# A graph layer and a mixture of experts: x also arrives transposed, and the row two edge groups share travels by DRAM

## The chip, the cores and the metric

The kernel runs on one core of one Trainium2 chip. Its time is that of one execution on the device, in microseconds (us).

## The reference, cut to what matters

The input `x` has 6250 nodes of 256 values. There are 100000 edges (`src`, `dst`), sorted by `dst`. All is float32.

```python
edge_index = jnp.stack([src, dst])
x = x + gnn(layernorm(x), edge_index, W, b)       # mean over a node's edges of h[src], then [h, mean] @ W.T + b
x = x + moe(layernorm(x)[None], ...)[0]           # norm again, 8 experts, the best 2 of them weighed by softmax

def gnn(h, edge_index, W, b):
    src, dst = edge_index
    msg_sum = segment_sum(h[src], dst, n)
    deg = segment_sum(ones, dst, n)
    agg = msg_sum / maximum(deg, 1)[:, None]
    return concatenate([h, agg], axis=1) @ W.T + b
```

## The kernel before, in words

**The start.** The nodes lie in 49 tiles of 128 rows (the last holds 106), taken in 13 blocks of four tiles (`TB`). The kernel multiplies x by the centred weights before it gathers anything: `z` is the normalised x times the half of W that the mean needs, and `u` is x plus the bias plus the normalised x times the other half. Both go to DRAM (`z_d`, `u_d`).

- `load_x` (L168) brings a block of x into `xt`, rows on the partitions; five blocks are asked for ahead, each later one after the block five before it.
- `z_statistics` (L201) takes mean and variance of each tile on DVE, 0.40 and 0.18 us each; `z_deviations` (L209) makes `rstd_x` of a block by a root on ACT (L146) and five small operations on DVE (L151 to L156).
- `z_block` (L215) handles a block in half blocks of two tiles. TensorE turns them with four transposes (L226), ACT copies the result into `x_t` (L227), and `product` (L192) multiplies `x_t` by `gc` (L197). ACT scales the product into `zt` (L237), and SP stores it in `z_d` (L240). The product of a half block is issued after the transposes of the next one (the list `pending`).
- From the fourth block on, a list of other steps is put between half blocks, one after each: constants, the second centring of weights, the turning of the edge lists into `src_i` and `dst_i`, the places of the windows (`place_windows`, `place_rows`) and checks that the edges are sorted.
- `u_stages` (L349) makes `u` in 26 tasks: load `xu`, add the bias (L356), multiply `x_t` by the other half (L197), add (L363), store (L367). Six of them stand ahead of the first edges and the others between them. `x_t` is kept until they are done.

**The edges.** The edges are cut in 784 groups of 128; 14 groups make a window, so there are 56 windows. One group is a step t of the program. POOL gathers the 128 rows of z that a group needs (`gather`, L533) into one of 16 buffers `xg`, 16 steps ahead of use. DVE compares each edge's `dst`, less the window's first node, with 0 to 127 and so makes `hot`, seven groups at once (L544, two buffers), and TensorE adds `hot` times `xg` up in `pS` (`add_edges`, L550), one product per step, with a 257th column of ones for the degree. A window covers the nodes from its first edge's on, 128 rows.

The last node of a window can have more edges in the next one; it is the next window's row 0. Before, this row goes over by a product. ACT copies `pS` into `sums` at the window's end (L556). DVE makes `move` from `last_row` (`carry`, L561), a matrix that picks the shared row and puts it in row 0, and TensorE adds `move` times the previous `sums` to `pS` after the seventh step of the window (L553). Float32 products show as two passes each in the profile.

`window_x1` (L572) divides by the degree and adds `u`, which `load_u` (L563) brings at step 13; the result goes to DRAM (L577).

**The experts.** Windows are grouped in nine chunks (4, then five of 8, then three of 4). For each chunk the tokens are normed, routed, sorted by products (L622) and copied into the experts' slots `xe` (`copy_runs` on ACT, L737, 64 copies for 8 windows). Then come 11 expert items (`expert_stages`, L753 to L810), the results go to `y_d`, and two gathers of POOL per window (L851) bring them back.

**The order.** All five queues (PE, DVE, ACT, POOL, SP) run in an order written out by hand. `after(t)` issues what is due at step t: `at(t, f)` puts a function at a step, `window_done` (L902) puts all that follows a window at fixed distances (`Steps`), and the expert tasks are spread at a rate worked out from their prices and deadlines. Each engine works through its own list in order.

Of the kernel before, what the change touches and what calls it, by code (L numbers as in the profile page):

```python
# [8 lines left out]
F32 = mybir.dt.float32  # L9
I32 = mybir.dt.int32  # L10
AF = mybir.ActivationFunctionType
ALU = mybir.AluOpType
# [5 lines left out]
P = 128  # L18
# [10 lines left out]


@with_exitstack
def gnn_ffn_kernel(ctx: ExitStack, tc: tile.TileContext, x, src, dst, gw_t, gb, gamma, beta,
                   wr, br, w1, b1, w2, b2, out):


# [52 lines left out]
    def slot_number(nw):  # L88
        return more_at(nw) + XT * P
# [6 lines left out]
    dram = ctx.enter_context(tc.tile_pool(name="dram", bufs=1, space=DRAM))  # L96
    z_d = dram.tile([HR, D], F32, name="z_d")
    u_d = dram.tile([HR, D], F32, name="u_d")
    y_d = [dram.tile([slot_number(nw), D], F32, name=f"y_d{i}") for i, (_, nw) in enumerate(chunks)]
    AR = -(-(N + EW) // P)  # L100
    x1_d = dram.tile([W * P, D], F32, name="x1_d")
# [79 lines left out]
    def rows_of(d, t0, n):  # L181
        return d[t0 * P:(t0 + n) * P, :].rearrange("(t p) d -> p t d", p=P)
# [26 lines left out]
    def z_deviations(t0):  # L209
        n = min(TB, NT - t0)  # L210
        a = small.tile([P, TB], F32, name="var_eps")
        nc.vector.tensor_scalar(a[:, :n], mvs[t0][:, :n, 1], EPS, None, op0=ALU.add)
        rsqrt(rstd_x[:, t0:t0 + n], a, root(a, n, TB), n, TB)

    def z_block(t0, pending, between):  # L215


        n = min(TB, NT - t0)
        xt, after = xts[t0], t0 + TB
        zt = early.tile([P, TB, D], F32, name="zt")  # L220
        for i in range(0, n, 2):
            m = min(2, n - i)
            pt = ps.tile([P, 2, KD, P], F32, name="pm")
            for j in range(m):
                for k in range(KD):
                    nc.tensor.transpose(pt[:, j, k, :], xt[:, i + j, k * P:(k + 1) * P], ident)  # L226
            nc.scalar.activation(x_t[:, t0 + i:t0 + i + m], pt[:, :m], AF.Copy)  # L227
            if t0 == i == 0:
                z_deviations(0)
            if after in blocks:  # L230
                z_statistics(after, range(i, i + 2))

            def rest(i=i, m=m):
                pz = product(t0 + i, m, KD)
                for j in range(m):
                    t = t0 + i + j
                    nc.scalar.activation(zt[:, i + j, :], pz[:, j, :], AF.Identity, scale=rstd_x[:, t:t + 1])  # L237
                if i + m == n or t0 >= blocks[-3]:
                    i0 = i if t0 >= blocks[-3] else 0
                    nc.sync.dma_start(rows_of(z_d, t0 + i0, i + m - i0), zt[:, i0:i + m, :])  # L240
            if pending:
                pending.pop()()
            pending.append(rest)
            if between:
                between.pop(0)()
        if after in blocks:
            z_deviations(after)
# [55 lines left out]


    start_i = edges.tile([1, W], I32, name="start_i")
    bases = edges.tile([P, 2, W + 1], F32, name="bases")
    last_row = edges.tile([P, W], F32, name="last_row")
    token = edges.tile([P, W], F32, name="token")
    tail_i = edges.tile([P, 2], I32, name="tail_i")
    wrongs = const.tile([1, 1], F32, name="wrongs")  # L310
# [1 line left out]
    def place_windows():  # L312
        rows = early.tile([1, 2, W + 1], F32, name="rows", bufs=1)
        nc.vector.tensor_copy(rows[:, 0, :W], base_i)
        nc.vector.memset(rows[:, 0, 0:1], 0.0)
        nc.vector.memset(rows[:, 0, W:], float(N))
        nc.vector.memset(rows[:, 1, W:], 0.0)
        nc.vector.tensor_tensor(rows[:, 1, :W], rows[:, 0, 1:], rows[:, 0, :W], op=ALU.subtract)

        furthest = early.tile([1, W], F32, name="furthest", bufs=1)  # L320
        nc.vector.tensor_scalar(furthest, cols[0:1, :W], float(P - 1), float(N - P), op0=ALU.mult, op1=ALU.min)
        nc.vector.tensor_tensor(start_i, rows[:, 0, :W], furthest, op=ALU.min)
        pb = ps.tile([P, 2, W + 1], F32, name="py", bufs=1)
        nc.tensor.matmul(pb, ones[0:1, :], rows, start=True, stop=True)
        nc.vector.tensor_copy(bases, pb)

    def place_rows():
        nc.vector.tensor_scalar(last_row, bases[:, 1, :W], lane, None, op0=ALU.is_equal)
        nc.vector.tensor_scalar(token, bases[:, 1, :W], lane, None, op0=ALU.is_gt)

        tail_f = early.tile([P, 2], F32, name="tail_f", bufs=1)
        nc.vector.tensor_tensor(tail_f[:, 0:1], bases[:, 0, W - 1:W], lane, op=ALU.add)
        nc.vector.tensor_scalar(tail_f[:, 1:2], tail_f[:, 0:1], float(N - 1), None, op0=ALU.min)
        nc.vector.tensor_copy(tail_i, tail_f)
# [51 lines left out]
        return [lambda t=t: step(t) for t in range(len(pairs) + 1)]  # L386

    blocks = list(range(0, NT, TB))
    pending = []
    mvs = {}  # L390
    base_i = early.tile([1, W], I32, name="base_i", bufs=1)
    xts = {t0: load_x(early, "xt", t0, min(TB, NT - t0), TB, 6) for t0 in blocks[:5]}
    edge_parts = load_edges()
    gb_sb = u_pool.tile([P, D], F32, name="gb_sb", bufs=1)
    nc.sync.dma_start(gb_sb, bass.AP(tensor=gb.tensor, offset=gb.offset, ap=[[0, P], [1, D]]))
# [14 lines left out]
    zero = u_pool.tile([CAP, D], F32, name="zero", bufs=1)  # L410
    nc.vector.memset(zero, 0.0)
# [135 lines left out]
    def add_edges(V, c):  # L547
        if c == 0:
            V.pS = ps.tile([P, DA], F32, name="pS")
        nc.tensor.matmul(V.pS, V.hot[c // HC][:, c % HC, :], xg[(V.g * C + c) % XG],  # L550
                         start=(c == 0), stop=(c == C - 1))
        if c == HC - 1 and V.g > 0:
            nc.tensor.matmul(V.pS, V.move, V.before.sums, start=False, stop=False)  # L553
# [437 lines left out]
    for index, (first, nw) in enumerate(chunks):  # L991
# [3 lines left out]
        for g in range(first, first + nw):  # L995
# [163 lines left out]
```

## Time and profile before

| | us |
|---|---|
| median of three runs | 1258.45 (1257.22, 1258.45, 1260.78) |
| the profiled execution | 1257.93 |
| its span | 1256.2 |
| PE busy | 1127.6 (90%) |
| POOL busy | 865.4 (69%) |
| DVE busy | 672.2 (54%) |
| ACT busy | 478.6 (38%) |
| first and last gather of z start (L533) | 76.6 and 1089.6 |
| last product of edges starts (L550) | 1115.6 |

The granted TensorE clock was 0.954 of full speed on average. The profile tells for each line and engine how long it was busy, how long the engine stood idle before it, and what ended that idle time. An arrow points to the releaser: `PE ph L753 <- ACT xe L737` says that TensorE waited at line 753 for what ACT wrote at line 737. PEld is the loading of weights into TensorE, which overlaps its products. SP works only by issuing transfers and has no busy time. An engine's busy share leaves out what lies between two of its instructions, and a busy share over the whole span mixes stages with different limits.

### The profile page before, as it was taken

What the parts mean: (1) busy time and instruction counts of PE and PEld (TensorE: products, weight loads), DVE (VectorE), ACT (ScalarE), POOL (GpSimd) and SP (SyncE); (2) the same over time, 40 slices, a digit from 0 to 9 for tenths busy, and PEclk for the clock granted to TensorE, in tenths of its full rate; (3) what the DMA queues carried; (4) which work ended last, traced back from release to release, by engine and by line L of the source; (5) the groups of instructions that cost most, each with busy time, mean ns of one, the idle gap of its engine ahead of it and who ended that gap; (6) DMA issues with size and microseconds to landing.
All of it is one profiled execution on the core that took longest, in us unless ns stands there. A gap on an engine that the chain in (4) does not pass through costs nothing. (4 is left out here: it accounts for less than half of the span.)

```text
span 1256.2 us, 18368 instructions
## 1 busy us (share of the span) xinstructions
PE 1127.6 (90%) x5322; PEld 931.6 (74%) x5322; DVE 672.2 (54%) x2072; ACT 478.6 (38%) x1209; POOL 865.4 (69%) x911
## 2 busy tenths in 40 slices
PE   8888877888988999899998999899998999998782
PEld 6777744665656888688877888688877888877661
DVE  6856547353663447453563457443663646357541
ACT  5510013521165234733364333733365243533510
POOL 2047777777777777777777777777777777656652
PEclk9999978899888999899998999899999999999986
DMA  8569894444444454445444444444444555467673
GB/s 266 162 213 324 264 358 124 122 125 127 138 126 122 134 151 131 143 127 152 134 144 128 140 146 134 142 133 142 135 147 140 158 167 158 138 178 211 192 211 92
DMA packets 129682, 203.46 MB, mean 162 GB/s; under 512 B 21997, under 2 KB 98561, under 8 KB 129448
## 3 DMA queue, kind: packets, MB, share of 16 engines
q0 software_dynamic: 43104, 117.72, 33.1%
q1 hardware_dynamic: 79528, 75.59, 18.5%
q10 hardware_dynamic: 6944, 8.91, 2.1%
q8 instruction: 45, 0.74, 0.2%
q14 instruction: 61, 0.50, 0.1%
HBM read 155.84 MB, written 46.33 MB: 161 GB/s over the span
## 5 line engine op out<-in xcount | busy, mean ns | idle before, releaser
L533 POOL DMA_INDIRECT xg<-z_d,src_i x784 | 747.7, 954 | 298.3 <-issue 110.0
L550 PE MATMUL pS<-xg,hot 128*128 128x257 f32 x1568 | 439.4, 397 | 33.5 <-DMA xg<-z_d,src_i 30.2
L550 PEld LDWEIGHTS pS<-xg,hot 128*128 128x128 f32 x1568 | 293.9, 196 | 113.9 <-DMA xg<-z_d,src_i 61.9
L753 PE MATMUL ph<-xe,w_sb 128*128 128x256 f32 (+1 forms) x1152 | 224.8, 346 | 28.4 <-ACT xe L737 26.7
L753 PEld LDWEIGHTS ph<-xe,w_sb 128*128 128x128 f32 x1152 | 188.9, 199 | 50.3 <-ACT xe L737 29.5
L768 PE MATMUL py<-w_sb,hid 128*128 128x256 f32 x896 | 215.3, 385 | 6.7 <-DVE rows L772 6.7
L544 DVE TENSOR_TENSOR hot<-cols,rel 128x896 f32<-128x896 f32 x112 | 121.9, 1089 | 144.1 <-PE pS L550 140.2
L768 PEld LDWEIGHTS py<-w_sb,hid 128*128 128x128 f32 x896 | 171.8, 193 | 32.0 <-DVE rows L772 8.1
L760 ACT ACTIVATE hid<-ph,b_sb 128x256 f32<-128x256 f32 (+1 forms) x288 | 103.4, 426 | 224.3 <-PE ph L753 224.1
L737 ACT ACTIVATE xe<-xs x448 | 139.3, 311 | 57.9 <-ACT xe L737 35.9
L851 POOL DMA_INDIRECT xg<-y_d,rows_i x90 | 87.0, 967 | 64.3 <-issue 16.4
L772 DVE TENSOR_TENSOR rows<-py,b_sb 128x512 f32<-128x512 f32 x56 | 38.6, 688 | 127.2 <-PE py L768 127.2
L197 PE MATMUL ph<-gc,x_t 128*128 128x256 f32 x392 | 95.5, 389 | 12.1 <-DVE u_t L363 8.7
L625 ACT ACTIVATE xs<-pm,beta_sb,gamma_sb 128x256 f32<-128x256 f32 x112 | 57.2, 561 | 96.1 <-PE pm L622 95.5
L556 ACT ACTIVATE sums<-pS 128x257 f32<-128x257 f32 x56 | 21.7, 388 | 188.3 <-PE pS L550 134.5
L197 PEld LDWEIGHTS ph<-gc,x_t 128*128 128x128 f32 x392 | 73.9, 194 | 24.5 <-DVE u_t L363 10.1
L622 PE MATMUL pm<-to,xn 128*128 128x256 f32 x224 | 58.9, 386 | 3.6 <-DVE end L685 2.6
L858 DVE SCALAR_TENSOR_TENSOR xg<-xg,w,xg 128x256 f32<-128x256 f32 x90 | 42.8, 483 | 35.1 <-DMA xg<-x_d 21.1
L803 PE MATMUL py<-w_sb,hid 128*128 x216 | 53.5, 392 | 5.9 <-ACT hid L797 4.6
L785 PE MATMUL ph<-w_sb,xe 128*128 x108 | 53.1, 615 | 4.3 <-DVE rows L789 3.8
L622 PEld LDWEIGHTS pm<-to,xn 128*128 128x128 f32 x224 | 42.5, 192 | 12.3 <-issue 5.6
L803 PEld LDWEIGHTS py<-w_sb,hid 128*128 128x128 f32 x216 | 41.0, 195 | 13.7 <-ACT hid L797 6.0
(178 smaller groups left out, 975.9 us busy)
## 6 DMA issues: line engine op xcount, KB each, us to landing
y_d<-rows SPq DMA_DIRECT2D x56, 256.0 KB
xg<-z_d,src_i POOLq DMA_INDIRECT x784, 2.8
w_sb<-w_dram ACTq DMA_DIRECT2D x16, 512.0 KB
x_d<-x SPq DMA_DIRECT2D x56, 128.0 KB
x<-u_d SPq DMA_DIRECT2D x55, 128.0 KB
xu<-x_dram SPq DMA_DIRECT2D x24, 256.0 KB
u_d<-u_t SPq DMA_DIRECT2D x24, 256.0 KB
xg<-x_d SPq DMA_DIRECT2D x45, 128.0 KB
```

Of the source, the lines that this page charges most:

```text
L197: nc.tensor.matmul(pz[:, i, :], x_t[:, t0 + i, k, :], gc[:, k0 + k, :], start=(k == 0), stop=(k == KD - 1))
L533: nc.gpsimd.indirect_dma_start(out=xg[(g * C + c) % XG][:, :D], out_offset=None, in_=z_d[:, :], in_offset=bass.IndirectOffsetOnAxis(ap=src ...
L544: nc.vector.tensor_tensor(hot, col[:, None, :].to_broadcast([P, HC, P]), V.rel[:, c:c + HC, None].to_broadcast([P, HC, P]), op=ALU.is_equal)
L550: nc.tensor.matmul(V.pS, V.hot[c // HC][:, c % HC, :], xg[(V.g * C + c) % XG], start=(c == 0), stop=(c == C - 1))
L622: nc.tensor.matmul(px[:, k, :], G.xn[i][:, k * P:(k + 1) * P], G.one_hot[i], start=True, stop=True)
L625: nc.scalar.activation(xs[:, at:at + 2 * P], px[:, k, :], AF.Identity, bias=beta_sb[:, k:k + 1], scale=gamma_sb[:, k:k + 1])
L737: nc.scalar.activation(K.xe[:, :, bass.ds(v[2 * i], CAP)], src[:, :, bass.ds(src_at, CAP)], AF.Copy)
L753: nc.tensor.matmul(ph[:, i, a * S:(a + 1) * S], w1_sb[:, U.e + a, k, c * P:(c + 1) * P], K.xe[:, k, (U.e + a) * S:(U.e + a + 1) * S], star ...
L760: nc.scalar.activation(U.hid[:, c, a * S:(a + 1) * S], ph[:, i, a * S:(a + 1) * S], AF.Gelu, bias=b1_sb[:, U.e + a, c:c + 1])
L768: nc.tensor.matmul(U.py[:, h, :], U.hid[:, c, h * P:(h + 1) * P], w2_sb[:, U.e + h * UE // 2, c, :], start=(c == 0), stop=(c == KH - 1))
L803: nc.tensor.matmul(py[:, 0, :], T.hid[:, c, :P], w2_sb[:, bass.ds(T.e, 1), c, :].rearrange("p a d -> p (a d)"), start=(c == 0), stop=(c == ...
L851: nc.gpsimd.indirect_dma_start(out=V.y2[r], out_offset=None, in_=y_d[K.index][:, :], in_offset=bass.IndirectOffsetOnAxis(ap=G.rows[:, r, i ...
```

## The change

The host hands over a second copy of x, `x_cols`, in which each 128x128 block of x is transposed; it is the same data in another order. `x_t` is loaded from it, 512 KB per block, beside the load of `xt`. The transposes and ACT's copies out of PSUM are gone, and so is `pending`: a half block's product, scaling and store follow each other. Loads run four blocks ahead instead of five, and `zt` has three buffers instead of two. The first block's deviations come ahead of its products.

`carry`, `last_row` and the product L553 are gone. At a window's end DVE adds `V.before.row` to row 0 of `pS` (`shared_row`). One step later ACT copies `pS` into `sums` (one buffer instead of two), at step 4 of the next window SP stores `sums` in one of two DRAM tiles `sums_d`, and at step 8 SP reads the number of the shared row from `span_i` into a register and loads this row of 257 values into `row`, where the next window's addition finds it.

```diff
-    def z_block(t0, pending, between):
+    def z_block(t0, between):
         n = min(TB, NT - t0)
-        xt, after = xts[t0], t0 + TB
-        zt = early.tile([P, TB, D], F32, name="zt")
+        after = t0 + TB
+        zt = early.tile([P, TB, D], F32, name="zt", bufs=3)
         for i in range(0, n, 2):
             m = min(2, n - i)
-            pt = ps.tile([P, 2, KD, P], F32, name="pm")
+            pz = product(t0 + i, m, KD)
             for j in range(m):
-                for k in range(KD):
-                    nc.tensor.transpose(pt[:, j, k, :], xt[:, i + j, k * P:(k + 1) * P], ident)
-            nc.scalar.activation(x_t[:, t0 + i:t0 + i + m], pt[:, :m], AF.Copy)
-            if t0 == i == 0:
-                z_deviations(0)
+                t = t0 + i + j
+                nc.scalar.activation(zt[:, i + j, :], pz[:, j, :], AF.Identity, scale=rstd_x[:, t:t + 1])
+            if i + m == n or t0 >= blocks[-3]:
+                i0 = i if t0 >= blocks[-3] else 0
+                nc.sync.dma_start(rows_of(z_d, t0 + i0, i + m - i0), zt[:, i0:i + m, :])
             if after in blocks:
                 z_statistics(after, range(i, i + 2))
-            def rest(i=i, m=m):
...
-            if pending:
-                pending.pop()()
-            pending.append(rest)
             if between:
                 between.pop(0)()
...
-    last_row = edges.tile([P, W], F32, name="last_row")
+    span_i = edges.tile([1, W], I32, name="span_i")
...
+        nc.vector.tensor_scalar(span_i, rows[:, 1, :W], 0.0, float(P - 1), op0=ALU.max, op1=ALU.min)
...
-        nc.vector.tensor_scalar(last_row, bases[:, 1, :W], lane, None, op0=ALU.is_equal)
...
+    def load_block(t0):
+        n = min(TB, NT - t0)
+        xts[t0] = load_x(early, "xt", t0, n, TB, 6)
+        nc.sync.dma_start(x_t[:, t0:t0 + n], x_cols[:, t0:t0 + n])
...
-    xts = {t0: load_x(early, "xt", t0, min(TB, NT - t0), TB, 6) for t0 in blocks[:5]}
+    for t0 in blocks[:4]:
+        load_block(t0)
...
     z_statistics(0, range(TB))
+    z_deviations(0)
     for t0 in blocks:
-        z_block(t0, pending, steps if t0 >= blocks[3] else None)
-        ahead = t0 + 5 * TB
-        if ahead in blocks:
-            xts[ahead] = load_x(early, "xt", ahead, min(TB, NT - ahead), TB, 6)
-        elif t0 == blocks[-4]:
+        if t0 + 4 * TB in blocks:
+            load_block(t0 + 4 * TB)
+        elif t0 == blocks[-3]:
             u_tasks = u_stages()
-    pending.pop()()
+        z_block(t0, steps if t0 >= blocks[3] else None)
...
-        if c == HC - 1 and V.g > 0:
-            nc.tensor.matmul(V.pS, V.move, V.before.sums, start=False, stop=False)
-        if c == C - 1:
-            V.sums = work.tile([P, DA], F32, name="sums")
-            nc.scalar.activation(V.sums, V.pS, AF.Copy)
-    def carry(V):
+    def shared_row(V):
         if V.g > 0:
-            V.move = work.tile([P, P], F32, name="move")
-            nc.vector.tensor_scalar(V.move, col, 0.0, last_row[:, V.g - 1:V.g], op0=ALU.is_equal, op1=ALU.mult)
+            nc.vector.tensor_tensor(V.pS[0:1, :], V.pS[0:1, :], V.before.row, op=ALU.add)
+    def keep_sums(V):
+        V.sums = work.tile([P, DA], F32, name="sums", bufs=1)
+        nc.scalar.activation(V.sums, V.pS, AF.Copy)
+    def put_sums(V):
+        if V.g < W - 1:
+            nc.sync.dma_start(sums_d[V.g % 2], V.sums)
+    def share_row(V):
+        if V.g < W - 1:
+            r = nc.values_load(span_i[0:1, V.g:V.g + 1], engines=(ET.SP,), min_val=0, max_val=P - 1,
+                               skip_runtime_bounds_check_because="clamped to it")
+            V.row = work.tile([1, DA], F32, name="row", bufs=1)
+            nc.sync.dma_start(V.row, sums_d[V.g % 2][bass.ds(r, 1), :])
...
     def window_done(V, G, K, t):
...
+        shared_row(V)
+        at(t + 1, keep_sums, V)
+        at(t + 4, put_sums, V)
+        at(t + 8, share_row, V)
         at(t + S.x1, window_x1, V)
...
-                    carry(V)
...
+    def columns(x):
+        rows = np.concatenate([x, np.zeros((-len(x) % P, x.shape[1]), x.dtype)])
+        return rows.reshape(-1, P, x.shape[1] // P, P).transpose(3, 0, 2, 1)
...
+        "x_cols": columns(a["x"]),
```

More of the change, by code (lines that the diff above doesn't have):

```diff
@@ L31, in gnn_ffn_kernel @@
 @with_exitstack
-def gnn_ffn_kernel(ctx: ExitStack, tc: tile.TileContext, x, src, dst, gw_t, gb, gamma, beta,
+def gnn_ffn_kernel(ctx: ExitStack, tc: tile.TileContext, x, x_cols, src, dst, gw_t, gb, gamma, beta,
                    wr, br, w1, b1, w2, b2, out):
@@ L98, in gnn_ffn_kernel @@
     u_d = dram.tile([HR, D], F32, name="u_d")
+    sums_d = [dram.tile([P, DA], F32, name=f"sums_d{i}") for i in range(2)]
     y_d = [dram.tile([slot_number(nw), D], F32, name=f"y_d{i}") for i, (_, nw) in enumerate(chunks)]
@@ L213, in z_deviations @@
         rsqrt(rstd_x[:, t0:t0 + n], a, root(a, n, TB), n, TB)
-    def z_block(t0, pending, between):
+    def z_block(t0, between):
         n = min(TB, NT - t0)
-        xt, after = xts[t0], t0 + TB
-        zt = early.tile([P, TB, D], F32, name="zt")
+        after = t0 + TB
+        zt = early.tile([P, TB, D], F32, name="zt", bufs=3)
         for i in range(0, n, 2):
             m = min(2, n - i)
-            pt = ps.tile([P, 2, KD, P], F32, name="pm")
+            pz = product(t0 + i, m, KD)
             for j in range(m):
-                for k in range(KD):
-                    nc.tensor.transpose(pt[:, j, k, :], xt[:, i + j, k * P:(k + 1) * P], ident)
-            nc.scalar.activation(x_t[:, t0 + i:t0 + i + m], pt[:, :m], AF.Copy)
-            if t0 == i == 0:
-                z_deviations(0)
+                t = t0 + i + j
[3 more added lines that the diff above has]
+                nc.sync.dma_start(rows_of(z_d, t0 + i0, i + m - i0), zt[:, i0:i + m, :])
             if after in blocks:
                 z_statistics(after, range(i, i + 2))
-            def rest(i=i, m=m):
[L234 to L240, printed above, removed]
-            if pending:
-                pending.pop()()
-            pending.append(rest)
             if between:
@@ L388, in gnn_ffn_kernel @@
     blocks = list(range(0, NT, TB))
-    pending = []
-    mvs = {}
+    mvs, xts = {}, {}
+    def load_block(t0):
+        n = min(TB, NT - t0)
+        xts[t0] = load_x(early, "xt", t0, n, TB, 6)
+        nc.sync.dma_start(x_t[:, t0:t0 + n], x_cols[:, t0:t0 + n])
     base_i = early.tile([1, W], I32, name="base_i", bufs=1)
-    xts = {t0: load_x(early, "xt", t0, min(TB, NT - t0), TB, 6) for t0 in blocks[:5]}
+    for t0 in blocks[:4]:
+        load_block(t0)
     edge_parts = load_edges()
```

## The prediction

> **What bounds it now.** I read the page's busy shares first (the first line below), then PE and POOL stage by stage, since a share over the whole span doesn't say who waits. The last chain is no help: it holds only the final store. Next come the view of the gather line L533 and the tile view of its target `xg` by stages (columns: us, then PE, PEld, DVE, POOL busy and count):
>
> ```profile
> PE 1127.6 (90%) x5322; PEld 931.6 (74%) x5322; DVE 672.2 (54%) x2072; ACT 478.6 (38%) x1209; POOL 865.4 (69%) x911
> L533 POOL DMA_INDIRECT xg<-z_d,src_i x784: 942/946/1485, 76.6 to 1089.6; - x196
>   DVE rel L541: 57.3, 1
> 450.00:500.00 50.00, 21.03 (x80) 14.77 (x80) 0.00 (x0) 37.82 (x41) 1.00 0.47 139
> 850.00:900.00 50.00, 22.88 (x90) 16.41 (x88) 0.00 (x0) 37.90 (x40) 1.00 0.47 138
> ```
>
> POOL idles 57.3 us ahead of the first gather; from 76.6 us on a gather starts every 1.25 us (40 to 41 in 50 us: 0.95 busy, 0.30 to the next). At 69% "busy" POOL is full until the last gather at 1089.6. PE is full as well. Its waits from 443 to 583 us, one cycle of eight windows, and its timeline around one carry product:
>
> ```profile
> PE ph L753 <- ACT xe L737: 4.7, 1, 4.7
> 608.45 0.60 PE L550 MATMUL pS<-xg,hot 128*128 128x257 f32 x2
> 608.88 0.60 PE L553 MATMUL pS<-sums,move 128*128 128x257 f32 x2
> 609.31 1.03 PE L550 MATMUL pS<-xg,hot 128*128 128x257 f32 x4
> ```
>
> One wait of 4.7 us in 140, on ACT's copies of slots, and none on a gather. The next product starts 0.43 us after L553: that is what L553 takes out of PE's stream. L553's starts in windows 32, 40 and 48 (658.8, 798.9, 939.0) lie 140.1 us apart; POOL's 112 gathers take 140.0. The two keep step, and PE's lag shows which has room: L553 starts 9.5 us after the gather of its own step in window 30, 8.8 in window 32, but 3.3 in windows 11 and 14, where PE waits for gathers. So PE could run some 6 us nearer to POOL. From window 49 on the lag grows, to 22.0 at window 55: there PE alone sets the pace (98% busy from 1000 to 1100).
>
> The start, from the timeline (start, duration, engine):
>
> ```profile
> 9.30 0.17 DVE L212 TENSOR_SCALAR var_eps<-mv 128x4 f32<-128x4 f32 x1
> 12.88 0.17 DVE L212 TENSOR_SCALAR var_eps<-mv 128x4 f32<-128x4 f32 x1
> 42.96 0.16 DVE L212 TENSOR_SCALAR var_eps<-mv 128x4 f32<-128x4 f32 x1
> 44.37 0.20 ACT L146 ACTIVATE root<-var_eps 128x4 f32<-128x4 f32 x1
> 44.61 0.18 DVE L151 RECIPROCAL rstd_x<-root 128x4 f32<-128x4 f32 x1 [1.48 <-ACT root L146]
> ...
> 69.86 0.16 DVE L156 TENSOR_TENSOR rstd_x<-rstd_x,newton 128x1 f32<-128x1 f32 x1
> 70.02 1.39 ACT L237 ACTIVATE zt<-ph,rstd_x 128x256 f32<-128x256 f32 x3 [0.69 <-PE ph L197]
> 75.95 0.19 DVE L525 MEMSET xs<- 128x64 f32 x2 [5.45 <-DMA z_d<-zt]
> 76.58 1.16 POOL L533 DMA_INDIRECT xg<-z_d,src_i  x1 [57.32 <-DVE rel L541]
> ```
>
> A block of four tiles takes DVE 3.58 us (9.30 to 12.88) while nothing holds it up; often ACT's root comes late, behind `zt` that waits for PE (1.48 us at 44.61). The last store lands at about 75.95, and the first gather follows.
>
> **What the Trainium skill says.** *Perfetto Trace Analysis*, "GPSIMD Engine Instruction" and its SWDGE part: such an instruction ends when its descriptors are made, not when the data has moved. The trace agrees: 0.95 us on POOL, 2.8 to landing. So POOL's cadence is the making, and lighter DMA traffic wouldn't speed it. *DMA: Bandwidth & Descriptors*, "Anatomy of one DMA": about 2 us fixed for each transfer; here 2.8 for a gather, the price I use for each leg of the row's trip. The same page, "Where 436 GB/s comes from": a ceiling of 435 GB/s; no 2 us slice of the start passes 366. *TensorE: Matmul & The Clock Gate*, "The HAM clock gate": about 3.4 us of idling halves the clock. The trace agrees: after the 4.7 us wait eight passes take 3.78 us instead of 1.89.
>
> **The change, part by part.** *Start.* Gone: 98 transposes (25 half blocks at 0.57 us of weight loads, 14 us of PE) and 25 copies L227 (0.60 each, 15 us of ACT). PE and ACT fall off the path, DVE stays with its work: first `var_eps` 9.30; eleven more blocks at 3.58, 39.4; the last block, one tile, 1.9; the interposed steps 11.8 (constants 0.86, second centring 0.65, four index casts 2.64, window and row places 2.0, four comparisons 4.9, the rest 0.75); one stall beside a POOL cast, 1.5. Sum 63.9; with 0.95 for the root and Newton, 0.47 for one `zt`, 0.36 to issue, 4.2 to land and 0.6 to the gather: 70.5 against 76.58, **6 us earlier**. Added: 6.4 MB of transposed x. Moved in this stage: 6.4 x, 6.4 x_cols, 6.4 z, 2.2 for weights, edges, bias and the first xu, 21.4 MB. The loaded slices from 4 to 12 and 18 to 22 us moved 337 to 366 GB/s; at 345 that is 62 us from 2 on, so done in time, but barely: at 300 it takes 71, and 4 to 5 us of the 6 are lost. Thirteen more issues on SP at 0.4 us are 5 us of an idle queue; they stand in line with the stores of z, and in the built program each of SP's transfers waits for the one eight before it, so that eight at most are open, 2.7 blocks ahead at three per block. I take 6, bounds 0 and 8. All that follows is paced by POOL and moves along.
>
> *Carry.* Gone: L553 on PE, 55 at 0.43, and L561 on DVE, 55 at 0.34. Added on DVE: a one-partition addition of 257 elements in PSUM; L576 on 128 partitions takes 0.48, so 0.45. It stands at the window's end, where DVE must now wait for PE's last product; but the next `hot` product of DVE waited for that same product one step later, so little is new: behind it stand `hot`, needed by PE seven steps (8.7 us) on, and the window's statistics. The copy L556 stays, one step later. On SP per window: one store of 128 KB, one register load (0.27, L528), one issue of 1 KB, together about 1.1 us in 17.5; behind them stand the load of u (five steps later) and stores of y. POOL issues nothing new. DMA gets 7.2 MB more over 1000 us (147 GB/s become 154).
>
> What PE gains: from window 15 to 48, where it is full, 34 times 0.43 is 14.7; two windows in each of four cycles lie beside ACT's slot copies (31 us of unbroken ACT, ended by PE's one wait), so 8 times 0.43 only lengthens that wait, leaving 11. But POOL allows some 6 (lag 9.5 down to 3.3). Windows 49 to 55 add 7 times 0.43, 3.0, since PE alone paces them. Of the 9 I take **8**, 1 being lost to slow clock after the new short waits; bounds 3 and 9.5. The tail after PE's last edge product (1116 to 1256) has the same work in the same order: 0.
>
> Sum: 6 + 8 = 14. The profiled execution took 1257.9 (span 1256.2 and 1.7 around it), 0.5 under the median of 1258.45: 1243.9, so **1244**.
>
> **Rivals.** (a) *The carry hides behind POOL*: PE's records end by a model, and its real slack may be nothing; then only the start counts, 1252. For it: POOL's even 1.25 us. Against: PE's lag after window 49. (b) *The doubled x fills the DMA*: first gather still at 75 to 77, only PE's 8 remain, 1250. For it: 21.4 MB in 68 us needs 315 GB/s without a gap. Against: slices at 360. (c) *Slower: the row's trip binds.* Place: DVE's addition at each window's end. The chain is addition 0.45, copy 0.4, store 2.8, load 2.8, but SP issues them in its turn, at steps 4 and 8, behind stores that wait on DVE. A row later than 17.5 us after the previous end stops DVE; from 26 us on (17.5 and seven steps) PE lacks its second `hot`. Each microsecond beyond costs 55: 0.5 us gives 1272. Against: ten microseconds to step 8 and 3.5 for the load leave 4 even to DVE. (d) The trip's SP waits delay u's loads while the DMA is full (80 to 150 us), PE falls sixteen steps behind, and POOL stops; three windows at 4 us take back 12: 1256, no change.
>
> **Numbers.** Under 0.3%, some 4 us, this kernel can't be told from no change. Both gains: 0.59; (a) 0.13; (b) 0.13; (c) 0.08; (d) 0.07. Faster 0.84, the same 0.08 ((d) and the worse end of (a)), slower 0.08. The likeliest alone spans 1240 to 1248; with (a) and (b) whole the range is 1239 to 1255, leaving out (c), (d) and little else.
>
> **What would show it.** First gather near 70.5; no long ACT root waits at the start; gathers still 1.25 us apart; PE waiting again for gathers in windows 22 to 48; its last L550-type product near 1102 instead of 1115; the wait on ACT's copies near 5.5. Wrong if the addition's wait for `row` is long, if slices of the start stay at the DMA's limit up to the first gather, or if the lag stays at 9.

## The result, and the profile after

The changed kernel takes 1253.72 us (median of eight runs, 1252.23 to 1255.72), the kernel before 1257.49 in the runs beside them (eight, 1255.83 to 1260.78). The ratio is 0.9969, with a 95% interval of 0.9955 to 0.9982: faster by some 3.8 us, where 14.5 were forecast. The profiled execution took 1255.72 us, the longest of the eight; its span is 1253.9.

First the busy shares of the page of the changed kernel:

```profile
PE 1098.8 (88%) x5114; PEld 907.8 (72%) x5114; DVE 679.0 (54%) x2072; ACT 460.8 (37%) x1183; POOL 865.7 (69%) x911
```

TensorE has 29 us less to do, ACT 18 less, POOL the same. Much of TensorE's and ACT's work is gone, but little of the time. Next the view of the gather line (L527 now), then the gathers' target by stages (columns as before: us, then PE, PEld, DVE and POOL busy and count, clock, DMA):

```profile
L527 POOL DMA_INDIRECT xg<-z_d,src_i x784: 942/946/1407, 75.0 to 1087.4; - x196
...
  DVE rel L535: 52.6, 1
```

```profile
450.00:500.00 50.00, 20.97 (x82) 15.41 (x83) 0.00 (x0) 37.82 (x41) 1.00 0.53 144
850.00:900.00 50.00, 22.89 (x88) 15.77 (x86) 0.00 (x0) 38.03 (x40) 1.00 0.55 151
```

The first gather comes 1.6 us earlier instead of 6. POOL is as full as before, and its last gather stands 1012.4 us after the first (1013.0 before). TensorE's waits in the same cycle of eight windows, 443 to 583 us:

```profile
PE ph L758 <- ACT xe L742: 4.0, 1, 4.0
...
PE pS L544 <- DMA xg<-z_d,src_i: 0.3, 1, 0.3
```

It still waits once for ACT's copies, and now also for a gather, as was forecast; but the wait on ACT's copies is 4.0 us where 5.5 were forecast. The start, from the timeline (start, duration, engine):

```profile
9.35 0.17 DVE L213 TENSOR_SCALAR var_eps<-mv 128x4 f32<-128x4 f32 x1
12.94 0.17 DVE L213 TENSOR_SCALAR var_eps<-mv 128x4 f32<-128x4 f32 x1
...
43.41 0.16 DVE L213 TENSOR_SCALAR var_eps<-mv 128x4 f32<-128x4 f32 x1
45.26 0.84 ACT L226 ACTIVATE zt<-ph,rstd_x 128x256 f32<-128x256 f32 x2 [5.06 <-PE ph L198]
45.99 0.20 ACT L147 ACTIVATE root<-var_eps 128x4 f32<-128x4 f32 x1
46.23 0.18 DVE L152 RECIPROCAL rstd_x<-root 128x4 f32<-128x4 f32 x1 [2.66 <-ACT root L147]
...
74.24 0.19 DVE L519 MEMSET xs<- 128x64 f32 x2 [2.11 <-DMA z_d<-zt]
74.34 0.09 DVE L867 TENSOR_SCALAR hundreds<-cols 1x8 f32<-1x8 f32 x1
74.36 0.22 DVE L535 TENSOR_SCALAR rel<-dst_i,bases 128x14 f32<-128x14 int32 x1
74.61 1.09 DVE L538 TENSOR_TENSOR hot<-cols,rel 128x896 f32<-128x896 f32 x1
74.99 1.15 POOL L527 DMA_INDIRECT xg<-z_d,src_i  x1 [52.59 <-DVE rel L535]
```

Read the fourth to sixth line together: `zt` on ACT waits 5.06 us for TensorE, the root stands behind it in ACT's queue, and DVE waits 2.66 us for the root. The idling that was to go has grown. The product that `zt` waits for is in TensorE's timeline:

```profile
40.75 0.77 PE L313 MATMUL py<-rows,ones 1*128 1x114 f32 x2 [2.65 <-DVE rows L306]
41.44 5.49 PE L198 MATMUL ph<-gc,x_t 128*128 128x256 f32 x12
```

TensorE stood 2.65 us for DVE, and then twelve passes took 5.49 us. At full clock eight take 1.89, so these ran at about half.

A span is the sum of four stretches. This table, in us, holds every trace taken where the kernel before takes about 1258 us (the experiments are told below):

| kernel | first gather | to the last gather | to the last edge product | to the end | span |
|---|---|---|---|---|---|
| before | 76.6 | 1013.0 | 26.0 | 140.6 | 1256.2 |
| changed | 75.0 | 1012.4 | 25.2 | 141.4 | 1253.9 |
| e7, x transposed alone | 71.2 | 1010.7 | 26.0 | 142.2 | 1250.1 |
| e8, carry by DRAM alone | 76.2 | 1012.3 | 25.1 | 141.9 | 1255.6 |
| e12, changed, no carry at all | 73.1 | 1011.6 | 25.1 | 139.6 | 1249.5 |
| e6, changed, transposes added | 75.6 | 1013.7 | 25.1 | 142.4 | 1256.8 |
| e9, before, later additions | 77.3 | 1011.4 | 23.7 | 141.4 | 1253.8 |
| e5, changed, later additions | 73.4 | 1014.0 | 22.9 | 140.1 | 1250.4 |
| e10, changed, root split | 68.9 | 1012.8 | 25.1 | 141.1 | 1247.9 |
| e11, e5 and e10 together | 69.1 | 1013.8 | 20.3 | 140.3 | 1243.5 |
| e13, as e11, carry by product | 69.0 | 1013.4 | 23.9 | 140.0 | 1246.4 |
| e14, as e11, no carry at all | 69.2 | 1009.3 | 20.2 | 139.4 | 1238.1 |

Each row is one execution. The new start, unchanged in five of them (changed, e5, e7, e12 and, but for TensorE's added work, e6), puts the first gather anywhere from 71.2 to 75.6 us; a difference of a few us between two rows is not to be read alone.

### The profile page after: what moved, and what is told of

Read it like the earlier page. It is cut to its first block, busy times and chain, and to the rows that moved or that the text cites. A ratio compares the mean times of both kernels' runs of the same rounds, so it can differ in the third digit from the quotient of the medians.

```text
span 1253.9 us, 18359 instructions
## 1 busy us (share of the span) xinstructions
PE 1098.8 (88%) x5114; PEld 907.8 (72%) x5114; DVE 679.0 (54%) x2072; ACT 460.8 (37%) x1183; POOL 865.7 (69%) x911
## 5 line engine op out<-in xcount | busy, mean ns | idle before, releaser
L527 POOL DMA_INDIRECT xg<-z_d,src_i x784 | 748.4, 955 | 292.6 <-issue 110.6
L544 PE MATMUL pS<-xg,hot 128*128 128x257 f32 x1568 | 428.8, 395 | 43.9 <-DMA xg<-z_d,src_i 29.9
L773 PEld LDWEIGHTS py<-w_sb,hid 128*128 128x128 f32 x896 | 172.3, 194 | 33.2 <-DVE rows L777 9.2
L198 PE MATMUL ph<-gc,x_t 128*128 128x256 f32 x392 | 100.8, 412 | 13.6 <-DVE u_t L351 10.5
L198 PEld LDWEIGHTS ph<-gc,x_t 128*128 128x128 f32 x392 | 80.1, 208 | 30.0 <-DVE u_t L351 12.1
L550 DVE TENSOR_TENSOR pS<-pS,row 1x257 f32<-1x257 f32 x55 | 22.9, 417 | 116.1 <-PE pS L544 90.1
L627 PE MATMUL pm<-to,xn 128*128 128x256 f32 x224 | 59.2, 387 | 10.2 <-DVE rest L659 3.5
```

What stands on the lines that cost most here:

```text
L198: nc.tensor.matmul(pz[:, i, :], x_t[:, t0 + i, k, :], gc[:, k0 + k, :], start=(k == 0), stop=(k == KD - 1))
L527: nc.gpsimd.indirect_dma_start(out=xg[(g * C + c) % XG][:, :D], out_offset=None, in_=z_d[:, :], in_offset=bass.IndirectOffsetOnAxis(ap=src ...
L627: nc.tensor.matmul(px[:, k, :], G.xn[i][:, k * P:(k + 1) * P], G.one_hot[i], start=True, stop=True)
L773: nc.tensor.matmul(U.py[:, h, :], U.hid[:, c, h * P:(h + 1) * P], w2_sb[:, U.e + h * UE // 2, c, :], start=(c == 0), stop=(c == KH - 1))
```

## The experiments

### Part by part, where every kernel ran slower: e1 to e4

These four ran where the kernel before took 1459.57 us. TensorE stood idle for 277 to 288 us of their spans (128 in the trace of the kernel before, 155 in that of the changed one), 75 to 121 us of it without a cause that the profile names ("issue"). In e2 half of the edge products started 14.6 to 20.8 us behind their gathers, so that TensorE was mostly well behind POOL. They say little of a balance of POOL and TensorE. Why they are slow isn't known: the record gives their chip the same number as that of e10 to e12, where the kernel before took 1257.56.

e1 puts the product back, with `last_row`, `move` and the copy that it needs (carry as before, new start):

```diff
-        shared_row(V)
-        at(t + 1, keep_sums, V)
-        at(t + 4, put_sums, V)
-        at(t + 8, share_row, V)
...
+        if c == HC - 1 and V.g > 0:
+            nc.tensor.matmul(V.pS, V.move, V.before.sums, start=False, stop=False)
```

> The transposed x of the change alone; the shared row goes over by the product, as before. Theory (the new start brings about 1.6 us, since the first gather went from 76.6 to 75.0 us, and the new carry some 2 us, because its 5 us of PE are given back in windows 47 to 55): first gather at 75.0 us, about 1255.7 us, 1.8 below before. Rival A (the whole gain comes from the start, the carry brings nothing): 1253.7 us. Rival B (the carry by DRAM even costs, by its row transfers): 1253 us or less.

Measured: ratio 0.9974 (0.9952 to 0.9995).

e2 is the kernel before with `shared_row`, `keep_sums`, `put_sums` and `share_row` in place of `carry`.

> The carry by DRAM alone; the start transposes x on TensorE, as before. Theory: first gather at 76.6 us, the lag of the sums behind the gathers falls from 9.9 to about 5 us in windows 20 to 45, and the time is about 1255.3 us, 2.2 below before. Rival A (carry brings nothing): 1257.5 us. Rival B (its row transfers cost): 1258 us or more. If the 5 us lag gain were kept to the end: 1252 us.

Measured: 0.9996 (0.9973 to 1.0019).

e3 takes the first four lines of e1's diff out of the changed kernel and puts nothing in their place.

> The changed kernel with the carry left out altogether: no product, no kept sums on ACT, no put, no row load, no one-row addition, so the row that two groups share lacks its earlier edges. Theory (the PE time is given back by the waits for the gathered expert rows near the end, not by the row's trip): within 1 us of the changed kernel, 1252.7 to 1254 us, and windows 47 to 55 take about 185 us again. Rival (the puts, row loads and additions lengthen POOL's cadence from 1.252 to 1.255 us and hold DVE near the end): 1250 us, cadence back at 1.252 us, windows 47 to 55 at 182 us or less.

Measured: 0.9938 (0.991 to 0.9966).

e4 adds transposes to the start:

```diff
+            warm = ps.tile([P, DA], F32, name="pS")
+            for _ in range(2 * m):
+                nc.tensor.transpose(warm[:, :P], ident, ident)
             pz = product(t0 + i, m, KD)
```

> The changed kernel with two transposes of the identity per tile of x ahead of each z product, into a PSUM buffer that nobody reads: as many transposes on TensorE as the kernel before has in its start, with nothing waiting for them. Theory (z products at half the clock, with ACT's square root standing behind the scaling that waits for them, lost 3 to 4 us of the start): granted clock 0.9 or more from 20 to 70 us, products of 8 at 1.9 us throughout, first gather at 71 to 72.5 us, time 1250 to 1251.5 us. Rival (DVE's own sum or the transfers set the start): first gather at 75 us or later, 1253.7 us or more.

Measured: 1.0008 (0.998 to 1.0036). On the absolute times and on windows 47 to 55 none of these expectations can be judged, for there the bound is another. All four were run again where the kernel before takes about 1258 us, as e7, e8, e12 and e6.

### The wait for the gathered expert rows: e5 and e9

In windows 48 to 55 DVE adds the rows that POOL gathers from `y_d`. The view of that line in the changed kernel:

```profile
L863 DVE SCALAR_TENSOR_TENSOR o<-y,w,o x22: 464/484/486, 960.7 to 1095.5; 128x256 f32<-128x256 f32 x22
its engine sat idle before it (us, times) until:
  DMA y<-y_d,rows_i: 24.6, 10
```

Before it was 14.6 us in seven waits. e5 has these additions later:

```diff
-            adds.append((clock + 6.0, lambda K=K, j=j, V=V: add_rows(K, j, V)))
+            adds.append((clock + 11.5, lambda K=K, j=j, V=V: add_rows(K, j, V)))
```

> The changed kernel with DVE's additions of the gathered expert rows 5.5 us of planned work later after their gathers (11.5 instead of 6.0), so that DVE stands less at those gathers in windows 48 to 55, where it stood 24.6 us in ten waits. Theory (PE now runs nearer to POOL, so these gathers, queued 16 steps ahead, come later for PE and DVE, and that wait gives the carry's gain back): DVE's waits there below 10 us, windows 47 to 55 at 181 us instead of 185.5, a time 3 to 5 us below the changed kernel, a ratio to the kernel before of 0.993 to 0.994. Rival (the wait is off the path, POOL's own sum sets those windows): the ratio stays at 0.997.

Measured: 1248.94 us, ratio 0.9923 (0.9895 to 0.995). The wait in the same view of e5:

```profile
  DMA y<-y_d,rows_i: 3.4, 2
```

From ACT's copy of the sums of window 47 to that of window 55 it took 181.4 us instead of 185.5. The theory's numbers came, with a gain a little above the 3 to 5 us that it gave. But the same edit could be worth as much without the new carry, so e9 makes it in the kernel before.

> The kernel before with the additions of the gathered rows 5.5 us of planned work later, as in e5, and nothing else changed. Theory (the wait for these gathers matters because PE runs nearer to POOL with the new carry; before, TensorE's sum was the bound in these windows and DVE stood only 14.6 us there): ratio 0.9985 to 1.000. Rival (the later additions are worth as much with either carry, so e5 tells nothing of the carry): ratio 0.996 or less.

Measured: 1256.51 us, ratio 0.9983 (0.997 to 0.9996), 2.2 us. That is a little more than the theory gave and less than the rival's. With the DRAM carry the same edit moves the ratio by 0.0046 (changed kernel to e5) and by 0.0048 (e10 to e11 below), 5.8 and 6.0 us. That the wait costs more with the new carry is likely, not certain: both differences to e9 are about as large as their own uncertainty. Without the new carry it costs something too.

### Is the start slow because TensorE runs cold? e6

The kernel of e4 again.

> The same kernel as in e4, on a chip on which the kernel before takes about 1258 us. Theory (half clock in the start, with the square root behind the scaling, cost 3 to 4 us): clock 0.9 or more from 20 to 70 us, first gather at 71 to 72.5 us against 73.4 and 75.0 us in the two traces of the changed start so far, ratio to the kernel before 0.994 to 0.995. Rival (DVE's sum or the transfers set the start, and the added transposes only stand before the products): first gather 74 us or later, ratio 0.997 or more.

Measured: 1258.6 us, ratio 1.0002 (0.9984 to 1.002). The start by stages, columns us, then PE, PEld, DVE, ACT and POOL busy and count, clock, DMA share, GB/s; first the changed kernel, then e6:

```profile
20.00:40.00 20.00, 17.18 (x93) 13.46 (x91) 17.32 (x73) 8.06 (x22) 1.89 (x2) 1.00 1.07 392
40.00:60.00 20.00, 16.15 (x58) 12.97 (x58) 15.14 (x67) 5.43 (x16) 0.00 (x0) 0.83 0.75 264
60.00:75.00 15.00, 13.53 (x54) 10.94 (x54) 8.38 (x61) 5.15 (x15) 0.01 (x1) 0.89 0.56 184
```

```profile
20.00:40.00 20.00, 20.00 (x121) 16.47 (x120) 15.25 (x62) 6.48 (x18) 2.67 (x2) 1.00 1.06 385
40.00:60.00 20.00, 16.09 (x89) 13.62 (x87) 16.73 (x76) 6.84 (x19) 0.00 (x0) 1.00 0.77 276
60.00:75.00 15.00, 13.66 (x72) 11.48 (x72) 7.12 (x54) 4.39 (x13) 0.00 (x0) 1.00 0.57 184
```

The clock is full all through, the first gather comes at 75.6, and the whole gain of the change is gone. The added transposes stand ahead of the products just as the old ones did, so this run can't tell what the half clock alone costs, only that this way of avoiding it costs more than it saves. The kept traces say more. In the four with the new start as it is, the first gather follows the granted clock from 20 to 70 us:

| kernel | clock, 20 to 70 us | DVE's waits for the root | first gather |
|---|---|---|---|
| changed | 0.90 | 9.1 | 75.0 |
| e5 | 0.93 | 7.8 | 73.4 |
| e12 | 0.93 | 7.4 | 73.1 |
| e7 | 0.97 | 6.2 | 71.2 |

In e6, at full clock, the waits for the root are 6.8. With the old start the clock is 1.00 in all three traces (before, e8, e9). So the theory's 3 to 4 us may well be right for the trace of the changed kernel. Four traces in line are no experiment, though, and no run takes the half clock away from this start without adding work.

### The parts again: e7 and e8

> The transposed x alone, as in e1, the shared row by the product. Theory (start worth 1.6 to 3 us, carry 1 to 2 us without later additions): ratio to the kernel before 0.998 to 0.9985. Rival A (all from the start): 0.997. Rival B (nothing from the start): 1.000.

Measured: 1253.46 us, ratio 0.9967 (0.9955 to 0.998). Rival A came closest: the transposed x alone gives as much as the whole change. The two intervals are 0.0013 wide to each side, so some 2 us of a carry on top are not excluded.

> The carry by DRAM alone, as in e2, the start as before. Theory: lag of the sums behind the gathers about 5 us at its smallest in windows 20 to 45 instead of 9.9, ratio to the kernel before 0.998 to 0.999, since windows 47 to 55 give most of it back. Rival A (carry kept to the end): 0.995. Rival B (its row transfers cost): 1.001 or more.

Measured: 1257.89 us, ratio 0.9988 (0.9975 to 1.0002): 1.5 us or nothing. Carry kept to the end (0.995) is excluded; whether the little is a gain can't be told.

### Splitting root and reciprocal: e10, and with later additions, e11

There remains DVE's own queue. In its order a block's root follows the block's statistics, and the reciprocal follows at once, so DVE stands still during each trip over ACT. e10 lets it do two statistics of the next block in between:

```diff
-        rsqrt(rstd_x[:, t0:t0 + n], a, root(a, n, TB), n, TB)
+        r = root(a, n, TB)
+        return lambda: rsqrt(rstd_x[:, t0:t0 + n], a, r, n, TB)
...
         for i in range(0, n, 2):
             m = min(2, n - i)
+            if after in blocks:
+                z_statistics(after, range(i, i + 2))
+            if i == 0:
+                finish.pop()()
             pz = product(t0 + i, m, KD)
...
-            z_deviations(after)
+            finish.append(z_deviations(after))
```

> The changed kernel with the start's reciprocal and Newton steps put behind the first two row statistics of the next block, so that DVE works while ACT takes the square root. Theory (the start is set by DVE's queue, 47 us of work and 13 trips over ACT's root of 0.58 us each, 7.5 to 9.5 us of waiting, in the kernel before and in the changed one alike): the waits for the root fall below 2 us, the last block's variance at 60 to 62 us instead of 65 to 69, first gather at 66 to 69 us, and since POOL is full from there on, the gain comes through whole: ratio to the kernel before 0.991 to 0.994. Rival (transfers or the z products on TensorE set the start): first gather 71 us or later, ratio 0.996 or more.

Measured: 1248.64 us, ratio 0.9925 (0.9911 to 0.994). The timeline of e10, at the block that was shown above:

```profile
47.41 0.15 DVE L213 TENSOR_SCALAR var_eps<-mv 128x4 f32<-128x4 f32 x1
47.55 0.27 DVE L173 MEMSET xt<- 128x256 f32 x1
47.75 0.36 DVE L162 BATCH_NORM_STATS2 st<-xt 128x6 f32<-128x256 f32 x1
48.14 0.18 DVE L163 BATCH_NORM_AGGREGATE mv<-st 128x2 f32<-128x6 f32 x1
48.24 0.40 DVE L162 BATCH_NORM_STATS2 st<-xt 128x6 f32<-128x256 f32 x1
48.67 0.18 DVE L163 BATCH_NORM_AGGREGATE mv<-st 128x2 f32<-128x6 f32 x1
48.77 0.14 DVE L152 RECIPROCAL rstd_x<-root 128x4 f32<-128x4 f32 x1
```

No wait stands before the reciprocal any more. The first gather comes at 68.9, and the following stretches of the table keep their lengths, so the gain goes through, and the theory's numbers came. The waits for the root between first and last variance fell to 1.9 us, as expected; the last variance came at 61.9. With DVE off these trips the clock matters less: it is 0.97 in e10 and 1.00 in e11, and their first gathers come at 68.9 and 69.1.

> e10 and the later additions of e5 together. If the two are independent: first gather as in e10, additions' waits below 10 us, ratio 0.986 to 0.990, about 1243 us. Rival (with POOL earlier, the wait for the gathered rows comes back, or the last windows are POOL's own): no better than the better of e5 and e10, 0.992.

Measured: 1244.02 us, ratio 0.9877 (0.9858 to 0.9896). DVE's additions wait 10.0 us for their rows, at the theory's limit. The two edits add up, and this version beats both kernels, by 13.5 and by some 10 us of the medians (15.5 and 11.6 by the ratios).

### What is the row itself worth? e12, e13 and e14

> As e3: the changed kernel without any carry, so the shared row lacks its earlier edges. Theory (POOL's cadence of 1.25 us per gather sets the time from first gather to last, so neither TensorE's 0.43 us a window nor the row's trip decides more than the lag at the end): ratio 0.995 to 0.9975, within 2 us of the changed kernel. Rival (puts, row loads, additions cost on DVE, ACT and the queues): ratio 0.994 or less, POOL from first to last gather in 1009 us or less instead of 1012.4.

Measured: 1251.61 us, ratio 0.9952 (0.9937 to 0.9966). As the theory had it, without a carry of either kind the stretch after the last gather is still 25.1 us; the time is 2 us below the changed kernel, at the limit of what the theory allowed.

e13 and e14 are e11 with the product of e1, and with no carry.

> e11 with the product instead of the DRAM row: transposed x, split root, later additions. Theory (the carry's PE time was lost to the waits for gathered rows, so without them it counts): 3 us or more slower than e11, ratio to the kernel before 0.990 to 0.992. Rival (POOL's sum from first to last gather sets the time and TensorE's share is hidden under it): same as e11, 0.987 to 0.9885.

Measured: 1246.53 us, ratio 0.9906 (0.9887 to 0.9925); e11 had 0.9877. The points lie 3.6 us apart, as the theory wants, but the two intervals overlap.

> e11 with neither product nor row, so the shared row lacks its earlier edges. Theory (the row's trip is hidden): within 1 us of e11, ratio 0.987 to 0.9885. Rival (its addition on DVE, its copy on ACT behind the sums and its transfers cost 2 us or more, as e12 against the changed kernel hints): 0.986 or less.

Measured: 1241.07 us, ratio 0.9868 (0.9846 to 0.9891): 1.1 us below e11 by the ratios, which the intervals don't tell from nothing, and 3.0 by the medians. It falls between the theory and the rival.

## Why the prediction was wrong, point by point

**The start: 6 us forecast, 1.6 to 5.4 in four traces.** The failed step is "PE and ACT fall off the path, DVE stays with its work". Take the time from the first `var_eps` to the last and subtract DVE's waits for ACT's root in it:

| kernel | first to last variance | waits for the root | rest |
|---|---|---|---|
| forecast | 54.6 | | |
| changed | 59.5 | 9.1 | 50.4 |
| e5 | 58.0 | 7.8 | 50.2 |
| e7 | 56.3 | 6.2 | 50.1 |
| e12 | 57.6 | 7.4 | 50.2 |
| e10 | 52.4 | 1.9 | 50.5 |
| before | 57.0 | 5.2 | 51.8 (1.5 of it for TensorE's turned indices) |

The forecast is 63.9 less 9.3. Each of its eleven blocks at 3.58 us holds one short wait for the root, as in this line of the kernel before:

```profile
9.74 0.18 DVE L151 RECIPROCAL rstd_x<-root 128x4 f32<-128x4 f32 x1 [0.27 <-ACT root L146]
```

Without these, 3.0 us in all, it has 51.6 us of work; the rest is 50.1 to 50.5 with the changed start, so DVE's own sum was sized well. The root waits were not: 3.0 forecast, 6.2 to 9.1 measured with the new start as it is, more than the 5.2 before, with less work on both engines. By the order of ACT's queue, only the first half block's scaling stood ahead of the next root before, since products ran half a block late; now both halves' scalings stand ahead of it and wait for products just issued. An engine with less to do was later with the one thing that mattered, because of what stood ahead of it in its queue. The forecast also left out TensorE's clock in the start: with the transposes gone, TensorE has gaps there and its clock falls (table under e6). How much each of the two adds is not shown. e10 shows what the trips cost, though not why they grew: taking DVE off them, with no work removed, brings 5.5 us (0.9969 to 0.9925), and the first gather comes at 68.9, against 71.2 to 75.0 in the four traces.

From the last variance to the first gather 6.6 us were forecast and 5.8 to 6.2 measured, where the kernel before took 10.3. The start's gain lies here: the blocks before took 56.3 to 59.5 us, and 57.0 in the trace of before. That the number fits is luck: to the end of the last `zt` 1.4 us were forecast and 3.1 to 3.5 measured (the last root waits for ACT too), and from there to the gather 5.2 forecast and 2.7 measured. Against the kernel before, with 5.1 and 5.2, the last block's work gave 1.6 to 2.0 us and the sooner landing of the last store 2.5. The prediction held that landing at 4.2; why it fell is not shown.

That "all that follows is paced by POOL and moves along" was right: 1009 to 1014 us to the last gather whatever TensorE did. Rival (b), the doubled x fills the DMA, was not the cause, though slices of the start ran at 392 GB/s. DVE waited for no load of x in the changed start, nor TensorE for one of `x_cols`, and e10 comes 6 us earlier with the same transfers.

**The carry in windows 22 to 48: the small lag came, but the carry is not needed for it.** Here is the lag of a step's product behind its own gather, start to start, in us, as the mean over a window's 14 steps. The last column is the time, in us, that the trace shows TensorE at half clock between 400 and 940 us (windows 20 to 48):

| kernel | w24 | w29 | w37 | w45 | w48 | w50 | w52 | w54 | last step | half clock |
|---|---|---|---|---|---|---|---|---|---|---|
| before | 8.0 | 10.0 | 9.9 | 9.9 | 8.2 | 18.6 | 20.0 | 25.1 | 25.8 | 20.5 |
| e9, before, later additions | 5.3 | 6.7 | 5.7 | 5.5 | 3.9 | 14.1 | 15.0 | 20.4 | 23.5 | 10.2 |
| e7, x alone | 4.8 | 5.6 | 4.8 | 4.9 | 4.3 | 14.0 | 17.6 | 23.2 | 25.8 | 12.8 |
| e13, product, later additions | 7.8 | 9.1 | 8.8 | 8.2 | 6.5 | 17.3 | 18.4 | 23.1 | 23.7 | 17.0 |
| changed | 4.5 | 5.4 | 5.0 | 4.3 | 4.4 | 13.5 | 18.3 | 23.6 | 24.9 | 20.5 |
| e8, carry alone | 5.9 | 5.3 | 4.7 | 4.4 | 4.2 | 14.1 | 17.0 | 23.0 | 24.9 | 10.2 |
| e12, no carry | 4.0 | 4.0 | 4.8 | 4.1 | 3.7 | 13.3 | 17.9 | 23.0 | 24.9 | 10.4 |
| e5, DRAM row, later additions | 4.6 | 4.4 | 4.2 | 5.2 | 4.3 | 15.4 | 15.6 | 20.2 | 22.7 | 10.2 |
| e11, DRAM row, later additions | 4.4 | 4.2 | 4.6 | 4.3 | 3.9 | 12.3 | 12.7 | 17.7 | 20.1 | 11.7 |

No step's lag falls below 2.7 us, the shortest flight of a gather. The changed kernel's lag is 4 to 5 us below that of the trace of before, as forecast. But e9 is the kernel before, step for step, up to window 48, and its lag is 4 to 7 us there; e7 has the product and 4 to 6. So the 9.9 that the forecast started from is what one execution showed, and no property of that kernel. In the trace of before TensorE and POOL both take 140.1 us for a cycle of eight windows from window 32 to 48 (the prediction's 140.0 is 112 times a rounded 1.25), and in e9 TensorE takes 139.5 to 139.9: a trifle decides whether it catches up, and one profile could not show that. Among the four kernels with the product, the two with more time at half clock (20.5 and 17.0) have the large lag. The changed kernel has 20.5 too and keeps the small one, so the carry may make it safer; more is not shown.

**Windows 49 to 55: the step that failed most.** "There PE alone sets the pace" was read off a busy share of 98%, and it made me count the whole gain to the end. Against the trace of before, the changed kernel enters window 50 with 5.1 us in hand (13.5 against 18.6), and at the last step 0.9 is left: its last edge product starts at 1112.5 us, where 1102 was forecast. With no carry at all (e12) the lag is the same 24.9, and e7, with the product and a small lag too, ends at the 25.8 of before. Most of the 5.1 goes in windows 50 to 52, where the lag grows by 4.8 us instead of 1.4. TensorE's waits from 940 to 1110 us, first the changed kernel (before, the first of these lines was 4.6 us and the next two were absent):

```profile
PE ph L758 <- ACT xe L742: 3.0, 1, 3.0
PE pm L627 <- DVE rest L659: 2.1, 1, 2.1
PE pm L627 <- DVE to L620: 1.3, 1, 1.3
```

And of e11:

```profile
PE pm L630 <- DVE to L623: 1.7, 1, 1.7
```

The cause of the late DVE is on POOL and in DVE's timeline, both of the changed kernel:

```profile
956.69 0.95 POOL L527 DMA_INDIRECT xg<-z_d,src_i  x1 [0.30 <-issue]
957.94 0.95 POOL L856 DMA_INDIRECT y<-y_d,rows_i  x1 [0.30 <-issue]
```

```profile
960.71 0.48 DVE L863 SCALAR_TENSOR_TENSOR o<-y,w,o 128x256 f32<-128x256 f32 x1 [9.76 <-DMA y<-y_d,rows_i]
```

The gathers of expert rows stand in POOL's full queue, behind the edge gathers of 16 steps ahead, and come when POOL gets there: 957.9 here, 959.0 before. DVE reaches the addition early when TensorE, which paces it, runs early. It waits 9.8 us here and 6.2 before, and then the slots (`to`) and shares (`rest`) that TensorE needs are late. A lead over POOL's schedule is turned into a wait for POOL. e5, e9, e11 and e13 bear it out: with later additions the lag grows by 0.2 to 1.1 us over these windows. From e13 to e11 the carry then keeps 3.6 us to the last step (23.7 and 20.1), but from e9 to e5 only 0.8: e5 enters window 50 with 15.4 after a wait of 4.0 us for ACT's copies and a clock of 0.77 from 940 to 955 us (e11: 2.0 us and 0.94). So how much is kept is shown by one pair of traces, and by ratios whose intervals overlap (e11 and e13). So rival (a), the carry hides behind POOL, was right in effect, but by another road: not in the slack of the steady stretch, but by the second kind of gather on POOL.

**What was taken as free.** The row's trip is hidden nearly everywhere; the view of the one-row addition in the changed kernel:

```profile
L550 DVE TENSOR_TENSOR pS<-pS,row x55: 408/420/422, 130.9 to 1114.8; 1x257 f32<-1x257 f32 x55
its engine sat idle before it (us, times) until:
  PE pS L544: 90.1, 28
  DMA row<-sums_d: 25.9, 5
```

The estimate of 0.45 us for the addition is 0.42. The row itself was late five times, all by window 15 and 22 us of it by window 7 (the place of rival (d)); there POOL's lead over the kernel before did not shrink (1.9 us at window 2, 2.6 at window 15). Rival (c), the trip binding in every window, is excluded. POOL's stretch is 1013.2 us on average in the six traces with a DRAM row and 1011.6 in the six without; the two sets overlap (1012.3 to 1014.0 and 1009.3 to 1013.4), so that a cost of 1.6 us to POOL is likely but not shown. e12 and e14, 2 and 1 us below their partners, fit it. The Trainium skill, *Perfetto Trace Analysis*, "DMA Instruction — SWDGE (GPSIMD)", says that such an instruction ends when its descriptors are made. The runs agree with what was made of it: from window 21 to 47 the median step from one gather to the next is 1.250 to 1.254 us in all twelve traces, beside 138 to 146 GB/s of traffic in all. The tail, forecast at 0, went from 140.6 to 141.4.

In sum: of the forecast 6 us the start gave about 4 (e7), and of the forecast 8 the carry gave nothing that the runs can tell from zero, since the changed kernel and e7 tie at 0.997. What stays open is the row's own 1 to 2 us, how much of the start's longer root waits is the clock and how much the order on ACT, and why the last store landed sooner.

## What to carry to other kernels

When an engine at 98% busy loses work, ask what its next supplier is pinned to: here POOL's queue is a clock, and a lead over it is spent at the next thing that comes from it, so the wait must be moved together with the work. Work taken off an engine helps the path only if what the path needs stands early in that engine's queue; look for short trips to another engine and put independent work between asking and using. Before you take work off an engine, ask also whether the gaps that it leaves lower the engine's clock. And where two engines keep step within 0.1%, one trace doesn't tell which of them has room: profile the same kernel twice.

## What the runs showed of the hardware

- A wait of 2.09 us was followed by half-speed passes; the timeline of TensorE in the changed kernel:

```profile
991.81 1.20 PE L627 MATMUL pm<-to,xn 128*128 128x256 f32 x4 [2.09 <-DVE rest L659]
992.80 3.53 PE L773 MATMUL py<-w_sb,hid 128*128 128x256 f32 x8
...
997.90 1.89 PE L773 MATMUL py<-w_sb,hid 128*128 128x256 f32 x8
```

  The Trainium skill, *TensorE: Matmul & The Clock Gate*, "The HAM clock gate", gives about 3.4 us of idling. A shorter wait, some nine microseconds after another of 1.3, was enough here, and one of 2.65 in the start (shown in the section on the result); the measurement decides.
- From 20 to 45 us the changed kernel moved 394 GB/s on average, above the 366 that was the most of any 2 us slice of this start before; so that was no limit.
- The last store of z landed 1.9 us after its `zt` (72.3 to 74.2) where it had taken 4.5 before (71.4 to 75.9).
- In one group of runs (e1 to e4) every kernel took 16% longer, with TensorE's clock at 0.90 to 0.91 and more than twice the idle time of the kernel before, in part without a cause that the profile names. The record doesn't tell whether the chip or its condition differed.
